# One-hots of the graph matrix for 8 or 10 receiver ranges per VectorE operation

## Chip, cores and metric

The kernel runs on one core of a Trainium2 chip. The metric is the device time of one execution in microseconds; of several runs the median is given.

## What is computed

The reference is a graph network on 12,500 nodes of 64 features and 212,500 edges, sorted by receiver. Cut to what matters:

```python
h = maximum(layernorm(x), 0)
for i in range(3):                         # L0_gnn, relu after the first two
    agg = segment_sum(h[src], dst) / maximum(count(dst), 1)
    h = agg @ Wl[i] + h @ Wr[i] + b[i]
x = x + h
h = maximum(layernorm(x), 0)
e = segment_sum(edge_attr, dst) / maximum(count(dst), 1)
x = x + mlp(concatenate([e, h]))           # three layers, W0, W1, W2
```

The sums over senders are made as matrix products: the graph is written out as a matrix with a small count for each sender and receiver, and all of it is multiplied with the node rows.

## The kernel before

The nodes form 98 blocks of 128 (`NB`), taken as 49 pairs (`HP`). The work has a start and three stages, one for each layer; the edge sums and the last network are woven into the third.

**Start.** The receivers at the heads of the edge tiles are fetched to `heads_row`, copied by VectorE to `heads_f` and spread over the partitions by TensorE (L321) and ScalarE (L324) into `heads`. The node rows come in 14 loads `xb` (L476) through SP's queue; `normed` and `relu_parts` (L201 to L226) apply the layer norm and cut the result into bfloat16 parts. The first matrix is built meanwhile.

**Stage one** does two things at once: it builds the matrix and uses it for the first layer. It runs over 49 passes, `hp` from 0. In pass `hp`, `dense` (L229) makes 98 matmuls at L234 and 98 at L243, whose moving operand is the matrix `m` of this pair of receiver blocks. Between them `woven` (L287) sets "fills" at given shares of the pass: 26 pair steps and a store that make the matrix of pass `hp + 1`, and at shares 0.05 and 0.15 the end of the pass before, `conv`'s `turn` (L260, L264) and `mix` (L269, L273, then L277, L280 on VectorE) followed by `relu_parts`.

**A pair step** (`pair`, L434) treats two receiver ranges. A block has 26 ranges of at most five receivers (`QW`, `WD`), each with up to 128 edges, one edge per partition. For a range, VectorE compares a row of numbers with a number per partition: `c` (L439) has 245 columns and a one where the edge's sender block and receiver fall, `h` (L443) has 128 columns with the sender's place in its block, times a weight of 1 or 256. TensorE multiplies the two (L447), into one half of a PSUM tile `pb` (three of them), and ScalarE casts the pair's result into `m` (L450). `c` and `h` come from the pool `hot` with six buffers each. The numbers `lo`, `weight` and `col` are float32 tiles, one column for each range.

**The index.** `index(j)` (L335) prepares those numbers for four blocks: it scans `heads` (L340, 1664 elements), gathers edges by three indirect DMAs that GpSimd issues (L330), counts on VectorE (L350 to L391), passes five small matmuls (L397) and a transpose (L406) through TensorE, and unpacks the codes (L414 to L426). It is woven in at share 0.6 of each even pass up to 44. Two indices are made in the start.

**Stages two and three** load the stored matrices back (L559) and multiply them with 512 columns at once; they use no one-hots of the edited kind.

**What sets the order.** On TensorE the order is that in which the code issues (`manual_schedule`). On VectorE, ScalarE and the queues the framework's scheduler orders the instructions; each engine then runs its list in order, waiting on semaphores. Tiles come from pools: a tile that takes a buffer waits until its last reader is done, and so does a pool that takes memory of a closed one. Pools `idx`, `hot`, `ln` (for the layer norm), `heads` and `mats` (three matrices `m`) are open through stage one; the pool `row` of the head row is closed early.

Of the kernel before, what the change touches and what calls it, by code (L numbers as in the profile page):

```python
# [9 lines left out]
F32 = mybir.dt.float32  # L10
I32 = mybir.dt.int32
BF16 = mybir.dt.bfloat16
# [3 lines left out]
ALU = mybir.AluOpType  # L16
# [5 lines left out]
P = 128  # L22
D = 64
# [11 lines left out]
QW, Q5 = 26, 24  # L35
WD = 5
# [24 lines left out]
def in_order(  # L61
# [24 lines left out]
    nc = tc.nc  # L86
    NB, T, EP = sz.nb, sz.t, sz.ep
    NL = Wl.shape[0]
    assert NB % 2 == 0
    HP = NB // 2  # L90
    CW = HP * WD
    NG = -(-NB // 4)
    assert EP - sz.e >= EK and CW <= 256

# [33 lines left out]
    with tc.tile_pool(name="setup", bufs=1) as s:  # L128
        ic = iota(s, "ic", CW, 1)
        nc.vector.tensor_copy(iota_c, ic)  # L130
# [4 lines left out]
        q = s.tile([P, 1], F32, name="q")  # L135
# [9 lines left out]
        a = s.tile([P, 1], F32, name="a")  # L145
# [40 lines left out]
    parts = [const.tile([P, NB, 3 * D], BF16, name=f"parts{i}") for i in range(2)]  # L186
# [14 lines left out]
    def normed(pool, xb, n, bufs=None):  # L201

        m = pool.tile([P, n], F32, name="ln_m", bufs=bufs)
        nc.vector.tensor_reduce(m, xb, axis=AX.X, op=ALU.add)
        nc.vector.tensor_scalar(m, m, -1.0 / D, None, op0=ALU.mult)
        c = pool.tile([P, n, D], F32, name="ln_c", bufs=bufs)
        nc.vector.tensor_tensor(c, xb, m[:, :, None].to_broadcast([P, n, D]), op=ALU.add)
        sq = pool.tile([P, n, D], F32, name="ln_sq", bufs=bufs)
        nc.scalar.activation(sq, c, AF.Square)
        v = pool.tile([P, n], F32, name="ln_v", bufs=bufs)  # L210
        nc.vector.tensor_reduce(v, sq, axis=AX.X, op=ALU.add)
        nc.scalar.activation(v, v, AF.Sqrt, bias=eps_t, scale=1.0 / D)
        nc.vector.reciprocal(v, v)
        nc.vector.tensor_tensor(c, c, v[:, :, None].to_broadcast([P, n, D]), op=ALU.mult)
        return c

    def relu_parts(pool, o, to, bufs=None):

        n = o.shape[1]
        nc.scalar.activation(to[:, :, :D], o, AF.Relu)  # L220
        r = pool.tile([P, n, D], F32, name="rest", bufs=bufs)
        nc.vector.scalar_tensor_tensor(
            r, o, 0.0, to[:, :, :D], op0=ALU.max, op1=ALU.subtract
        )
        nc.scalar.copy(to[:, :, D : 2 * D], r)
        nc.vector.tensor_tensor(to[:, :, 2 * D :], r, to[:, :, D : 2 * D], op=ALU.subtract)  # L226
# [76 lines left out]
    with ExitStack() as s:  # L303
        idx = s.enter_context(tc.tile_pool(name="idx", bufs=2))
        ps_b = s.enter_context(tc.tile_pool(name="ps_build", bufs=3, space=PSUM))
        ps_i = s.enter_context(tc.tile_pool(name="ps_idx", bufs=1, space=PSUM))
        hot = s.enter_context(tc.tile_pool(name="hot", bufs=6))
        ln = s.enter_context(tc.tile_pool(name="ln", bufs=1))
        heads = s.enter_context(tc.tile_pool(name="heads", bufs=1)).tile([P, T], F32, name="heads")
        with tc.tile_pool(name="row", bufs=1) as r:  # L310
            heads_row = r.tile([1, T], I32, name="heads_row")
# [6 lines left out]
            for c in range(0, T, 512):  # L318
                n = min(512, T - c)
# [2 lines left out]
                    ph[:, :n], ones[:1, :], heads_f[:, c : c + n], start=True, stop=True  # L322
                )
                nc.scalar.copy(heads[:, c : c + n], ph[:, :n])  # L324
        mats = s.enter_context(tc.tile_pool(name="mats", bufs=3))

        tiles_d = dst.rearrange("(t e) o -> t (e o)", e=P)

# [6 lines left out]
        def index(j):  # L335
# [5 lines left out]
                lower, heads, n0, None, op0=ALU.is_lt, op1=ALU.add, accum_out=tile_of  # L341
# [9 lines left out]
                junk, ends, n0, None, op0=ALU.is_lt, op1=ALU.add, accum_out=in_tile  # L351
# [30 lines left out]
            own = 32 * min(4, NB - 4 * j)  # L382
            for k in range(1, 5):
# [3 lines left out]
                    op1=ALU.is_equal, accum_out=twins[:own, j, k - 1 : k],  # L387
# [8 lines left out]
            for d in range(WD):  # L396
# [11 lines left out]
            nc.vector.tensor_copy(ci, pi[:, 1, :])  # L408
            a = idx.tile([P, P], I32, name="a")
            b = idx.tile([P, P], I32, name="b")  # L410
            lo = idx.tile([P, P], F32, name="lo")
            weight = idx.tile([P, P], F32, name="weight")
            col = idx.tile([P, P], F32, name="col")
            nc.vector.tensor_scalar(a, ci, P - 1, None, op0=ALU.bitwise_and)  # L414
            nc.vector.tensor_copy(lo, a)
            nc.vector.tensor_scalar(
                b, ci, 7, 1, op0=ALU.logical_shift_right, op1=ALU.bitwise_and
            )
            nc.vector.tensor_scalar(weight, b, 255.0, 1.0, op0=ALU.mult, op1=ALU.add)
# [6 lines left out]
            nc.vector.scalar_tensor_tensor(col, a, float(WD), b, op0=ALU.mult, op1=ALU.add)  # L426
            return lo, weight, col

        def build(m, block, codes):

            lo, weight, col = codes
            off = P * (block % 2)

            def pair(q):  # L434
                pb = ps_b.tile([P, 2, 256], F32, name="pb")
                for i in range(2):
                    w = 32 * (block % 4) + q + i
                    c = hot.tile([P, CW], BF16, name="c")
                    nc.vector.tensor_scalar(  # L439
                        c, iota_c, col[:, w : w + 1], None, op0=ALU.is_equal  # L440
                    )
                    h = hot.tile([P, P], BF16, name="h")
                    nc.vector.tensor_scalar(  # L443
                        h, iota_l, lo[:, w : w + 1], weight[:, w : w + 1],
                        op0=ALU.is_equal, op1=ALU.mult,
                    )
                    nc.tensor.matmul(pb[:, i, :CW], h, c, start=True, stop=True)  # L447
                k = WD if q < Q5 else WD - 1
                o = off + WD * q - max(q - Q5, 0)
                nc.scalar.copy(  # L450
                    m[:, :, o : o + 2 * k].rearrange("p h (w d) -> p h w d", d=k),
                    pb[:, :, :CW].rearrange("p w (h d) -> p h w d", d=WD)[:, :, :, :k],
                )

            return [lambda q=q: pair(q) for q in range(0, QW, 2)]
# [26 lines left out]
        with tc.manual_schedule(engines={PE}):  # L482
            codes[1] = index(1)
            m, fills = matrix(0)
            for f in fills:
                f()
            later = []
            for hp in range(HP):
                fills = list(later)
                if hp + 1 < HP:  # L490
                    m_next, more = matrix(hp + 1)
                    fills += [((i + 0.5) / len(more), f) for i, f in enumerate(more)]
                if hp % 2 == 0 and hp // 2 + 2 < NG:
# [12 lines left out]
                if hp + 1 < HP:  # L506
                    m = m_next
            for _, f in later:
                f()


    with ExitStack() as s:
# [4 lines left out]
        n = T // 4  # L517
# [29 lines left out]
    with ExitStack() as s:  # L547
        mats = s.enter_context(tc.tile_pool(name="mats2", bufs=9, reuse_waits="tile"))
# [14 lines left out]
        with tc.manual_schedule(engines={PE}):  # L563
            later = []
            for g in range(NG):
                j0, n = 4 * g, min(4, NB - 4 * g)
# [116 lines left out]
            for g in range(NG):  # L683
                j0, n = 4 * g, min(4, NB - 4 * g)
# [575 lines left out]
```

## Time and profile before

| | |
|---|---|
| median of 3 runs | 3512.63 us (3511.34 to 3512.82) |
| profiled execution | 3514.05 us |
| its span on the core | 3512.3 us, mean granted clock 0.992 |
| TensorE busy | 3350.0 us, 95% of the span |
| VectorE busy | 2111.3 us, 60% |
| ScalarE busy | 1196.0 us, 34% |
| start, to the first L234 | 0 to 104.0 us |
| stage one | 104.0 to 1450.7 us |
| stages two and three | 1450.7 us to the end |

A line of the groups gives source line, engine, operation, output and inputs, shapes and count; then the busy time in all and the mean length of one in ns; then the idle time of the engine just before them and what ended it. A line of the timeline gives the start and the length in us, then the same; a bracket at its end is the engine's wait and what ended it. Busy time is summed without overlap, while lengths of neighbouring operations can overlap, so the distance from start to start tells what one costs its engine.

### The profile page before, as it was taken

The numbers are of one execution on the slowest core, as the hardware profiler recorded it, in microseconds if no ns is written. First come the engines' busy times: TensorE is split into PE (matmuls) and PEld (weight loads), VectorE is DVE, ScalarE is ACT, GpSimd is POOL, SyncE is SP. The second block draws the span as 40 slices with busy tenths as digits, with TensorE's granted clock in tenths as the row PEclk, the third lists the DMA queues.
The fourth block names the chain that finished last, engine by engine and source line by source line (L and its number), as shares of the span: only waits on it lengthen the run. The fifth ranks groups of instructions, "written<-read, shape, count | busy, mean of one in ns | idle before, by whom it ended". The sixth has DMA issues, their size and how long they took to land.

```text
span 3512.3 us, 69396 instructions
## 1 busy us (share of the span) xinstructions
PE 3350.0 (95%) x26430; PEld 2019.0 (57%) x26430; DVE 2111.3 (60%) x9072; ACT 1196.0 (34%) x2101; POOL 750.7 (21%) x482
## 2 busy tenths in 40 slices
PE   1899999999999999999999999979999999999998
PEld 0566777777777777555454545544555555555555
DVE  8999999999999999300000000035556555555554
ACT  4555555555555555100000000022322322322232
POOL 1000000000000000000000000055555565555562
PEclk9999999999999999999999999989999999999999
DMA  2222222332223223645454545455455555555551
GB/s 45 115 116 118 115 116 115 137 129 115 115 120 146 115 111 134 233 155 220 155 212 165 202 176 191 170 218 181 176 182 211 204 206 181 176 183 211 204 193 53
DMA packets 168554, 555.12 MB, mean 158 GB/s; under 512 B 57793, under 2 KB 60386, under 8 KB 161938
## 3 DMA queue, kind: packets, MB, share of 16 engines
q1 hardware_dynamic: 133232, 478.53, 35.7%
q0 software_dynamic: 19648, 66.90, 5.6%
q10 hardware_dynamic: 15330, 5.16, 0.6%
q8 instruction: 208, 3.41, 0.4%
q14 instruction: 136, 1.11, 0.1%
HBM read 389.97 MB, written 160.56 MB: 157 GB/s over the span
## 4 chain that ended last, share of the span: by engine, by line
PE 84%; DVE 10%; issue 4%; DMA 1%; ACT 1%; POOL 0%; ACTq 0%; SPq 0%; DVEq 0%; POOLq 0%
PE p L234 40%; PE p L243 24%; PE pb L447 8%; PE pe L631 5%; DVE h L443 2%; DVE c L439 2%; PE po L273 2%; PE po L269 2%; PE pt L260 2%; DVE own L627 2%; PE ph L666 1%; PE mo L674 1%; DVE lower L340 0%; DVE junk L385 0%; PE mt L659 0%
## 5 line engine op out<-in xcount | busy, mean ns | idle before, releaser
L234 PEld LDWEIGHTS <-parts 128*128 128x128 bf16 x9702 | 937.2, 99 | 584.7 <-issue 46.2
L234 PE MATMUL p<-t,parts 128*128 128x512 fp8e3 (+1 forms) x4900 | 1106.7, 376 | 4.6 <-DMA t<-mat 4.6
L450 ACT CAST m<-pb 128x490 uint16<-128x490 f32 (+1 forms) x1274 | 717.4, 563 | 537.3 <-PE pb L447 534.4
L627 DVE TENSOR_SCALAR own<-iota_l,eplace 128x128 bf16<-128x128 bf16 x1862 | 548.2, 353 | 401.8 <-PE pe L631 401.4
L443 DVE TENSOR_SCALAR h<-iota_l,lo,weight 128x128 bf16<-128x128 bf16 x2548 | 779.8, 306 | 0.0
L439 DVE TENSOR_SCALAR c<-iota_c,col 128x245 bf16<-128x245 bf16 x2548 | 716.5, 281 | 10.9 <-PE pb L447 5.5
L243 PEld LDWEIGHTS <-parts 128*64 128x64 bf16 x9702 | 494.1, 109 | 387.8 <-issue 185.1
L234 PE MATMUL p<-m,parts 128*128 128x256 fp8e3 x4802 | 652.3, 273 | 0.6 <-ACT m L450 0.6
L243 PE MATMUL p<-t,parts 128*64 128x512 fp8e3 (+1 forms) x4900 | 584.4, 378 | 0.0
L447 PE MATMUL pb<-c,h 128*128 128x245 bf16 x2548 | 499.0, 274 | 52.4 <-DVE h L443 35.0
L248 DVE TENSOR_TENSOR agg<-e,p 128x256 f32<-128x256 f32 (+1 forms) x99 | 54.4, 549 | 603.2 <-PE p L243 600.3
L243 PE MATMUL p<-m,parts 128*64 128x256 fp8e3 x4802 | 409.3, 281 | 0.0
L602 POOL DMA_INDIRECT raw<-in_edge_dram,mine x98 | 93.7, 956 | 1124.9 <-DMA t<-mat 1098.6
L447 PEld LDWEIGHTS <-h 128*128 128x128 bf16 x2548 | 205.6, 98 | 204.0 <-DVE h L443 148.9
L613 POOL TENSOR_TENSOR erest<-raw,cut 128x1216 f32<-128x1216 f32 x98 | 244.2, 2492 | 202.2 <-issue 198.1
L631 PE MATMUL pe<-cut,own 128*128 128x192 bf16 x1862 | 227.0, 248 | 34.9 <-DVE own L627 17.5
L631 PEld LDWEIGHTS <-own 128*128 128x128 bf16 x1862 | 151.3, 98 | 166.4 <-issue 58.6
L615 POOL TENSOR_TENSOR cut<-erest,cut 128x1216 bf16<-128x1216 f32 x98 | 244.6, 2496 | 11.2 <-ACT cut L614 2.6
L612 ACT CAST cut<-raw 128x1216 bf16<-128x1216 f32 x98 | 118.1, 1205 | 275.6 <-PE pe L631 266.0
L277 DVE TENSOR_TENSOR o<-po,inv 128x128 f32<-128x128 f32 (+1 forms) x99 | 35.1, 354 | 271.8 <-PE po L273 271.6
L614 ACT CAST cut<-erest 128x1216 bf16<-128x1216 f32 x98 | 118.1, 1205 | 225.6 <-POOL erest L613 225.6
L330 POOL DMA_INDIRECT to<-in_dst_dram,at_i x25 | 23.6, 946 | 709.6 <-DVE at_i L358 595.8
(143 smaller groups left out, 1666.8 us busy)
## 6 DMA issues: line engine op xcount, KB each, us to landing
t<-mat SPq DMA_DIRECT2D x686, 448.0 KB, 6.1
mat<-m SPq DMA_DIRECT2D x49, 3136.0 KB, 10.0
xb<-in_x_dram SPq DMA_DIRECT2D x14, 224.0 KB, 2.7
xr<-in_x_dram ACTq DMA_DIRECT2D x24, 128.0 KB, 2.2
out_dram<-o SPq DMA_DIRECT2D x24, 128.0 KB, 2.0
raw<-in_edge_dram,mine POOLq DMA_INDIRECT x98, 5.4
eto<-in_dst_dram,mine POOLq DMA_INDIRECT x98, 3.7
here<-in_dst_dram ACTq DMA_DIRECT2D x4, 208.0 KB, 5.5
```

The costliest lines, as they stand in the source:

```text
L234: nc.tensor.matmul(p1, rows[:, i, : 2 * D], at(i), start=i == 0, stop=i == NB - 1)
L243: nc.tensor.matmul(p2[half], rows[:, i, 2 * D :], at(i), start=i < 2, stop=i >= NB - 2)
L439: nc.vector.tensor_scalar(c, iota_c, col[:, w : w + 1], None, op0=ALU.is_equal)
L443: nc.vector.tensor_scalar(h, iota_l, lo[:, w : w + 1], weight[:, w : w + 1], op0=ALU.is_equal, op1=ALU.mult,)
L447: nc.tensor.matmul(pb[:, i, :CW], h, c, start=True, stop=True)
L450: nc.scalar.copy(m[:, :, o : o + 2 * k].rearrange("p h (w d) -> p h w d", d=k), pb[:, :, :CW].rearrange("p w (h d) -> p h w d", d=WD)[:, : ...
L612: nc.scalar.copy(cut[:, :, :D], raw)
L613: nc.gpsimd.tensor_tensor(rest, raw, cut[:, :, :D], op=ALU.subtract)
L614: nc.scalar.copy(cut[:, :, D : 2 * D], rest)
L615: nc.gpsimd.tensor_tensor(cut[:, :, 2 * D :], rest, cut[:, :, D : 2 * D], op=ALU.subtract)
L627: nc.vector.tensor_scalar(o, iota_l, place[:, k : k + 1], 1.0 / UNIT, op0=ALU.is_equal, op1=ALU.mult,)
L631: nc.tensor.matmul(state["p"], o, cut[:, k, :], start=k == 0, stop=k == EK - 1)
```

## The change

For each block, VectorE makes the one-hots in three batches of 10, 8 and 8 ranges, each with three operations: one `tensor_tensor` comparison for all `c`, one for all `h`, and one `tensor_tensor` product of `h` with the weights, in place. One operand is the row of numbers, repeated for each range; the other is the code of the range, repeated along the row. Codes now stand twice, in bfloat16, so that they are read as rows of two neighbours; `lo`, `weight` and `col` are twice as long. `CW` becomes 246; the matmul still reads 245 columns. `hot` has two buffers of each kind, each for ten ranges.

Memory is laid out anew: `ln` is now opened after `row` is closed and is closed itself before `mats` is opened, so that `mats` comes to lie where `ln` was, and `ln` where `row` was. The code of the layer norm is moved, not altered.

```diff
-    CW = HP * WD
+    CW = 2 * (-(-HP * WD // 2))
...
-        hot = s.enter_context(tc.tile_pool(name="hot", bufs=6))
-        ln = s.enter_context(tc.tile_pool(name="ln", bufs=1))
+        hot = s.enter_context(tc.tile_pool(name="hot", bufs=2))
...
-        mats = s.enter_context(tc.tile_pool(name="mats", bufs=3))
...
-            lo = idx.tile([P, P], F32, name="lo")
-            weight = idx.tile([P, P], F32, name="weight")
-            col = idx.tile([P, P], F32, name="col")
+            lo = idx.tile([P, P, 2], BF16, name="lo")
+            weight = idx.tile([P, P, 2], BF16, name="weight")
+            col = idx.tile([P, P, 2], BF16, name="col")
+            twice = lambda t: t[:, :, None].to_broadcast([P, P, 2])
...
-            nc.vector.tensor_copy(lo, a)
+            nc.vector.tensor_copy(lo, twice(a))
...
+            cuts = [(0, 10), (10, 18), (18, QW)]
+            ready = {}
+
+            def hots(q0, q1):
+
+                n = q1 - q0
+                w = 32 * (block % 4) + q0
+                pairs = lambda t, k: t.rearrange("p (k t) -> p k t", t=2)[:, None].to_broadcast(
+                    [P, n, k // 2, 2]
+                )
+                own = lambda t, k: t[:, w : w + n, None, :].to_broadcast([P, n, k // 2, 2])
+                split = lambda t: t[:, :n].rearrange("p w (k t) -> p w k t", t=2)
+                c = hot.tile([P, 10, CW], BF16, name="c")
+                nc.vector.tensor_tensor(
+                    split(c), pairs(iota_c, CW), own(col, CW), op=ALU.is_equal
+                )
+                h = hot.tile([P, 10, P], BF16, name="h")
+                nc.vector.tensor_tensor(split(h), pairs(iota_l, P), own(lo, P), op=ALU.is_equal)
+                nc.vector.tensor_tensor(split(h), split(h), own(weight, P), op=ALU.mult)
+                for i in range(n):
+                    ready[q0 + i] = (h[:, i, :], c[:, i, : HP * WD])
 
             def pair(q):
+                for cut in cuts:
+                    if q == cut[0]:
+                        hots(*cut)
                 pb = ps_b.tile([P, 2, 256], F32, name="pb")
                 for i in range(2):
-                    w = 32 * (block % 4) + q + i
-                    c = hot.tile([P, CW], BF16, name="c")
-                    nc.vector.tensor_scalar(
-                        c, iota_c, col[:, w : w + 1], None, op0=ALU.is_equal
-                    )
-                    h = hot.tile([P, P], BF16, name="h")
-                    nc.vector.tensor_scalar(
-                        h, iota_l, lo[:, w : w + 1], weight[:, w : w + 1],
-                        op0=ALU.is_equal, op1=ALU.mult,
-                    )
-                    nc.tensor.matmul(pb[:, i, :CW], h, c, start=True, stop=True)
+                    h, c = ready[q + i]
+                    nc.tensor.matmul(pb[:, i, : HP * WD], h, c, start=True, stop=True)
...
-        def start_rows(a0):
-            n = min(LG, NB - a0)
-            xb = ln.tile([P, n, D], F32, name="xb", bufs=2)
-            nc.sync.dma_start(xb, xv[:, a0 : a0 + n, :])
-            relu_parts(ln, normed(ln, xb, n), parts[0][:, a0 : a0 + n, :])
-
         codes[0] = index(0)
-        for a0 in range(0, NB, LG):
-            start_rows(a0)
+        with tc.tile_pool(name="ln", bufs=1) as ln:
+            for a0 in range(0, NB, LG):
+                n = min(LG, NB - a0)
+                xb = ln.tile([P, n, D], F32, name="xb", bufs=2)
+                nc.sync.dma_start(xb, xv[:, a0 : a0 + n, :])
+                relu_parts(ln, normed(ln, xb, n), parts[0][:, a0 : a0 + n, :])
+        mats = s.enter_context(tc.tile_pool(name="mats", bufs=3))
```

In the changed kernel the comparisons stand at L448 (`c`) and L452 (`h`), the product at L453, the matmul at L464 and the cast at L467; lines below the `hot` pool and above L406 move up by one or two.

More of the change, by code (lines that the diff above doesn't have):

```diff
@@ L418, in index @@
             )
-            nc.vector.tensor_scalar(weight, b, 255.0, 1.0, op0=ALU.mult, op1=ALU.add)
+            nc.vector.tensor_scalar(weight, twice(b), 255.0, 1.0, op0=ALU.mult, op1=ALU.add)
             a = idx.tile([P, P], I32, name="a")
@@ L425, in index @@
             nc.vector.tensor_scalar(b, ci, 14, None, op0=ALU.logical_shift_right)
-            nc.vector.scalar_tensor_tensor(col, a, float(WD), b, op0=ALU.mult, op1=ALU.add)
+            nc.vector.scalar_tensor_tensor(
+                col, twice(a), float(WD), twice(b), op0=ALU.mult, op1=ALU.add
+            )
             return lo, weight, col
@@ L432, in build @@
             off = P * (block % 2)
+            cuts = [(0, 10), (10, 18), (18, QW)]
[11 more added lines that the diff above has]
+                    split(c), pairs(iota_c, CW), own(col, CW), op=ALU.is_equal
+                )
+                h = hot.tile([P, 10, P], BF16, name="h")
[3 more added lines that the diff above has]
+                    ready[q0 + i] = (h[:, i, :], c[:, i, : HP * WD])
             def pair(q):
+                for cut in cuts:
+                    if q == cut[0]:
+                        hots(*cut)
                 pb = ps_b.tile([P, 2, 256], F32, name="pb")
                 for i in range(2):
-                    w = 32 * (block % 4) + q + i
-                    c = hot.tile([P, CW], BF16, name="c")
-                    nc.vector.tensor_scalar(
-                        c, iota_c, col[:, w : w + 1], None, op0=ALU.is_equal
-                    )
-                    h = hot.tile([P, P], BF16, name="h")
-                    nc.vector.tensor_scalar(
-                        h, iota_l, lo[:, w : w + 1], weight[:, w : w + 1],
-                        op0=ALU.is_equal, op1=ALU.mult,
-                    )
-                    nc.tensor.matmul(pb[:, i, :CW], h, c, start=True, stop=True)
+                    h, c = ready[q + i]
+                    nc.tensor.matmul(pb[:, i, : HP * WD], h, c, start=True, stop=True)
                 k = WD if q < Q5 else WD - 1
@@ L451, in pair @@
                     m[:, :, o : o + 2 * k].rearrange("p h (w d) -> p h w d", d=k),
-                    pb[:, :, :CW].rearrange("p w (h d) -> p h w d", d=WD)[:, :, :, :k],
+                    pb[:, :, : HP * WD].rearrange("p w (h d) -> p h w d", d=WD)[:, :, :, :k],
                 )
```

## The prediction, made before the changed kernel was run

> **What bounds the kernel now.** I read the slices of the page first, then the groups, then two windows, then the timeline around one stall. The slices:
>
> ```profile
> PE   1899999999999999999999999979999999999998
> ...
> DVE  8999999999999999300000000035556555555554
> ...
> PEclk9999999999999999999999999989999999999999
> ```
>
> TensorE is at nine tenths all through; VectorE only until about 1400 us, the stage that builds the graph matrix. Only that stage runs the edited code. Its groups:
>
> ```profile
> L443 DVE TENSOR_SCALAR h<-iota_l,lo,weight 128x128 bf16<-128x128 bf16 x2548 | 779.8, 306 | 0.0
> L439 DVE TENSOR_SCALAR c<-iota_c,col 128x245 bf16<-128x245 bf16 x2548 | 716.5, 281 | 10.9 <-PE pb L447 5.5
> ...
> L447 PE MATMUL pb<-c,h 128*128 128x245 bf16 x2548 | 499.0, 274 | 52.4 <-DVE h L443 35.0
> ```
>
> The durations overlap: 281 + 306 = 587 ns per range would be 30.5 us for the 52 ranges of a pass, and a pass takes some 27. The timeline gives the true spacing:
>
> ```profile
> 599.77 0.28 DVE L439 TENSOR_SCALAR c<-iota_c,col 128x245 bf16<-128x245 bf16 x1
> ...
> 599.96 0.30 DVE L443 TENSOR_SCALAR h<-iota_l,lo,weight 128x128 bf16<-128x128 bf16 x1
> ...
> 600.18 0.28 DVE L439 TENSOR_SCALAR c<-iota_c,col 128x245 bf16<-128x245 bf16 x1
> ```
>
> c holds VectorE 0.195 us and h 0.222, so a range costs 0.417. Now two odd passes side by side (columns: window, its length, busy time of PE, PEld, DVE, ACT, POOL):
>
> ```profile
> 697.10:724.50 27.40, 26.48 (x264) 19.61 (x262) 27.15 (x128) 15.68 (x30) 1.89 (x2) 1.00 0.30 123
> ...
> 1240.80:1267.10 26.30, 26.30 (x265) 19.52 (x264) 25.67 (x124) 15.68 (x30) 0.00 (x0) 1.00 0.30 124
> ```
>
> The first loses 0.92 us of PE busy time, the second none: 26.26 us is what TensorE needs when nothing holds it. What held the first:
>
> ```profile
> 711.16 1.94 DVE L340 TENSOR_SCALAR_CACHE_REDUCE lower<-heads,node 128x1664 bf16<-128x1664 f32 x1
> ...
> 713.78 0.56 PE L447 MATMUL pb<-c,h 128*128 128x245 bf16 x2 [0.92 <-DVE c L439]
> ```
>
> The 1.94 us count of the next index stands between one-hots, and the pair's matmul waits. So TensorE bounds this stage, and VectorE, nearly full, adds short stalls.
>
> **What the Trainium skill says.** "VectorE: DVE Perf Modes", The perf-mode tier table, gives tensor_tensor on bf16 in SBUF two results a cycle at best. The trace has no such operation: every tensor_tensor in it has a float32 side. "Vector Engine (DVE) Microarchitecture Reference", 5.1 Performance modes, asks for 2-byte types, innermost step 1 and over one element, and says that rows of two elements and a row read again do run at two. The built operands are of that kind: iota in runs of 246 or 128 repeated per range, each code as a row of two repeated. 5.2 of that page, Measured stream behaviour, charges a source that hops every 4-byte word up to 1.73 ns a column; whether re-reading one word counts so no run shows, though L207, which re-reads one float32 per group, took 417 ns beside 418 to 458 for same-size operations without that.
>
> **The change, part by part.** Rate: L226 takes 282 ns for 128 elements and 618 for 448, so 1.05 ns an element at one a cycle; its spacing of 0.20 us for 128 leaves 67 ns fixed. c at 245 elements fits two a cycle: 245 x 0.525 + 67 = 195.
>
> 1. Removed: 26 c and 26 h per block, 26 x 0.417 = 10.84 us.
> 2. Added, at 0.525 ns: c for 10, 8, 8 ranges, 1.36 + 1.10 + 1.10; h compare and h multiply 0.74 + 0.61 + 0.61 each; the multiply waits for the compare's end, about 0.09 (306 - 222) three times. Sum 7.7 us. Bounds: 14.3 + 0.3 at one element a cycle; below, 7.4 without the waits. I take 7.7. A pass of two blocks sheds 6.2 us of VectorE.
> 3. lo, weight and col twice as long: +0.3 to +0.5 us per index, 25 of them, under TensorE's work. Without that cover, 13 us in all.
> 4. TensorE's order and matmuls, and ACT's casts, are unchanged. So a pass can only come down to its floor. By the starts of L234 in the trace, passes 0 to 47 take 1322.5 us. Floors: 26.26 without an index, 27.18 with one (its five small matmuls, the transpose and a 0.25 us wait), 25 x 26.26 + 23 x 27.18 = 1281.6. **At most 40.9 us** to win: some 26 in passes 0 to 9, 15 in the odd passes 11 to 35 at 1.16 each.
> 5. New wait: with two buffers a batch's c waits until TensorE has read the batch before the last. Behind it on VectorE are agg (L248), L277, L280 and the index chain. In a floor pass the batches are first read at 0.45, 6.83, 10.83, 14.84, 19.18 and 23.54 us. By hand on the built order, with an index: agg at 0.2 to 0.6, batch two ready 2, counts and the 1.94 us scan to 5.5, L277 from 5.6, a wait for the gather (issued about 3.7, 2.5 to land) to 6.3, batch three ready 9.6 (read 10.8), batch four 14.2 (14.8), batch five 16.7 (19.2), batch six 22.7 (24.4, the index moves it), next batch one 26.2 (27.6). All are in time, the tightest by 0.6 us. I keep 3 us for stalls: bounds 0 and, if 0.7 us were lost in each of 23 passes, 16. Loop: -38.
> 6. Start. Before, VectorE ends the layer norm at 97.3, and the first dense matmul comes 6.7 later:
>
> ```profile
> 97.63 5.81 PE L447 MATMUL pb<-c,h 128*128 128x245 bf16 x14 [0.57 <-DVE h L443]
> 104.01 1.01 PE L234 MATMUL p<-m,parts 128*128 128x256 fp8e3 x4 [0.57 <-ACT m L450]
> ```
>
> Three things move. (a) The ln tiles now lie where the head row lay, so SP's x loads wait for the head matmuls (last ends 16.4 us, before L204 started at 10.4), and VectorE, out of setup work by 14, idles until the heads are copied: about +2. (b) The built order puts seven head scans before the norm's end, not three, and 3 more chains at least partly: 4 x 1.94 + about 9 = 16.7 us; against that two batches (5) replace 39 ranges (39 x 0.417 = 16.3): +5. (c) mats overlies ln, so all 26 casts of matrix 0 come after the norm, not 7. ACT spaces them 0.465 (95.65 to 96.12 below), 12.1 us, and twice a multiply is queued behind the next c, which waits for a buffer, 1.3 to 2 us: 15.7 in place of 6.7, and some 0.5 to the first cast and matmul: about +10.
>
> ```profile
> 95.65 0.57 ACT L450 CAST m<-pb 128x490 uint16<-128x490 f32 x1 [0.33 <-PE pb L447]
> 96.12 0.56 ACT L225 CAST parts<-rest 128x448 bf16<-128x448 f32 x1
> ```
>
> Sum +17; bounds +10 (a hidden, no queue) and +24. Index work done early wins nothing later, since TensorE bounds the passes.
> 7. After 1450 us no line changes; SP's t loads wait on other addresses, and I cost that at nothing: behind it lie nine buffers, and the existing first wait there is 4.6 us. If that grew, it would double at worst.
>
> Sum: -38 + 17 = **-21 us**. The profiled execution took 3514.05 (span 3512.3), 1.4 over the median 3512.63. 3512.6 - 21 = 3492 us.
>
> **Rivals.** *Start hidden* (A): the batches make the start's VectorE work shorter than I count, start about +2, loop -39: 3476. For it: VectorE is the engine of the first 100 us. Against: the casts cannot start earlier. *Edges stall* (B): 0.7 to 1 us at one late batch in each pass, loop about -15: 3512 to 3516. For it: a margin of 0.6 us in step 5. Against: VectorE's slack of 5 us a pass recovers. *Slow reads* (C), the one that ends slower: the repeated two-element rows run at one a cycle. Then a pass costs VectorE 2 x 14.6 + 5.3 (other work: 27.4 less 52 x 0.417, less half a microsecond idle) = 34.5 against 27.2 now, 48 x 7.3 = 350, plus the start: about 3880. It decides from 10.7 us a block (26.7 - 5.3 over two); the 1.73 ns price, two elements to a column, would give about 12.2 and so 3650. For it: no such operation in the trace. Against: the page's measured rows. That the change does not do what it says is excluded by the built program: 3 c, 3 h and 3 multiplies a block.
>
> **Numbers.** Forecast (start +10 to +24, loop -25 to -41) 0.62; A 0.10; B 0.14; C 0.14. Measurements of this kernel tell about 0.2% (7 us) from no change. Faster: forecast, A and 0.04 of B, 0.76; same 0.10 from B; slower C. Own range of the forecast 3481 to 3512; with A and most of B 3475 to 3514, which leaves out C and a rest.
>
> **What would show it.** c of 2460 elements near 1.4 us apart from the next, not 2.65; odd passes at 26.26 from the first on; the first L234 at about 121 us; L467's casts all after the last L225. Wrong: passes over 27.5, waits of L464 for the multiply in every pass, or a first L234 near 105.

## The result, and the profile after

| | before | after |
|---|---|---|
| median | 3512.73 us (4 runs, 3511.34 to 3516.27) | 3566.57 us (4 runs, 3564.33 to 3567.49) |
| ratio, 95% interval | | 1.0151, 1.0133 to 1.0168 |
| span of the profiled execution | 3512.3 us | 3562.5 us |
| VectorE busy | 2111.3 us | 1831.2 us |
| first L234 | 104.0 us | 124.7 us |
| passes 0 to 47 | 1322.5 us | 1352.8 us |
| pass 48 | 24.2 us | 23.8 us |
| from there to the end | 2061.7 us | 2061.2 us |

The kernel became slower by 1.5%, where 0.6% faster was forecast. The spans differ by 50.2 us: 20.7 in the start, 30.3 in passes 0 to 47, -0.3 in pass 48 and -0.5 behind it. A pass is counted from its first L234 to that of the next. The slices of the changed kernel:

```profile
PE   0699999999999999999999999989999999999998
...
DVE  8777777777677676400000000026555565555554
```

VectorE got its room: 7 tenths where it had 9. TensorE has next to no work in the first slice and needs longer to the end of the stage. The groups of stage one, by shape, show that the batches cost what was forecast:

```profile
L448 DVE TENSOR_TENSOR c<-iota_c,col 128x1968 bf16<-128x1968 bf16 x195 | 230.5, 1182 | 108.8 <-PE pb L464 108.7
...
L448 DVE TENSOR_TENSOR c<-iota_c,col 128x2460 bf16<-128x2460 bf16 x97 | 139.7, 1440 | 61.9 <-PE pb L464 61.8
...
L453 DVE TENSOR_TENSOR h<-h,weight 128x1280 bf16<-128x1280 bf16 x97 | 79.9, 824 | 2.6
...
L363 DVE TENSOR_SCALAR place<-to,node 128x128 f32<-128x128 int32 x20 | 5.7, 286 | 85.6 <-DMA to<-in_dst_dram,at_i 85.6
```

From 1968 to 2460 elements the time grows by 258 ns, 0.524 ns an element, half of the 1.05 ns that the prediction took from L226. What is new is the idle time of the last line: `place` works for 5.7 us in all, and VectorE waits 85.6 us before it for the gathered receivers `to`. In the kernel before, VectorE never waited before the same operation:

```profile
L365 DVE TENSOR_SCALAR place<-to,node 128x128 f32<-128x128 int32 x25 | 7.0, 278 | 0.0
```

Pass by pass (windows of three passes; length, then busy time of PE, PEld, DVE, ACT, POOL; clock, DMA share, GB/s):

```profile
691.40:718.70 27.30, 27.05 (x271) 19.82 (x270) 19.88 (x42) 15.69 (x30) 0.00 (x0) 1.00 0.28 119
718.70:747.80 29.10, 26.77 (x264) 19.27 (x262) 21.36 (x48) 15.56 (x30) 2.83 (x3) 1.00 0.30 119
...
1291.40:1317.70 26.30, 26.30 (x264) 19.44 (x263) 17.36 (x28) 15.68 (x30) 0.00 (x0) 1.00 0.30 124
```

The even pass stands at its floor of 27.24 us. The odd pass with the three gathers (POOL x3) takes 29.1, and the odd pass without them 26.3. Over passes 0 to 47 the floors (26.33 without an index, 27.24 with one) sum to 1284.8 us; 68.0 us are stalls, 67 of them in the 20 odd passes 1 to 39. The timeline of the odd pass from 718.70:

```profile
718.62 0.32 SPq L483 DMA_DIRECT2D mat<-m  x1
...
721.74 0.15 DVE L356 TENSOR_SCALAR at_i<-begins 128x1 int32<-128x1 f32 x1
...
722.17 0.94 POOL L328 DMA_INDIRECT to<-in_dst_dram,at_i  x1 [52.27 <-DVE at_i L356]
...
724.40 0.29 DVE L277 TENSOR_TENSOR o<-po,inv 128x128 f32<-128x128 f32 x1 [0.27 <-PE po L273]
...
728.89 0.29 DVE L363 TENSOR_SCALAR place<-to,node 128x128 f32<-128x128 int32 x1 [4.19 <-DMA to<-in_dst_dram,at_i]
729.09 0.28 DVE L280 TENSOR_TENSOR o<-o,po 128x128 f32<-128x128 f32 x1
...
729.40 0.31 ACT L220 ACTIVATE parts<-o 128x128 bf16<-128x128 f32 x1 [3.89 <-DVE o L280]
729.62 0.55 ACT L467 CAST m<-pb 128x490 uint16<-128x490 f32 x1
730.22 0.37 PE L464 MATMUL pb<-c,h 128*128 128x245 bf16 x2 [1.51 <-ACT m L467]
...
732.13 0.39 PE L464 MATMUL pb<-c,h 128*128 128x245 bf16 x2 [0.77 <-DVE h L453]
```

Read it as a chain. The 3.1 MB store of the finished matrix is issued at the pass's start. VectorE, ahead of its old place, reaches `at_i` 3 us later, so the gather is issued while the store runs. `place` is a few operations further in VectorE's order, after the 1.94 us scan and directly behind L277; VectorE stands 4.19 us before it, waiting for the gather. Behind it stand L280 and the next batch of `c`. ScalarE's L220 waits for L280, and the casts that free `pb` stand behind L220. TensorE then loses 1.51 us to a late cast and 0.77 to a late product. Over passes 0 to 47 these two waits of TensorE make 46 of the 67 us (us, times, longest):

```profile
PE pb L464 <- ACT m L467: 31.9, 20, 2.9
PE pb L464 <- DVE h L453: 13.9, 18, 0.8
```

In the kernel before, in the odd pass from 697.1, `at_i` came 14 us into the pass, when the store had ended, and `place` 16.7 us behind it:

```profile
711.10 0.15 DVE L358 TENSOR_SCALAR at_i<-begins 128x1 int32<-128x1 f32 x1
...
727.76 0.28 DVE L365 TENSOR_SCALAR place<-to,node 128x128 f32<-128x128 int32 x1
```

Why the gather is late is in the DMA view, cut at 727.3 us (queue: packets, MB, share of 16 engines). From 719.4 to 727.3:

```profile
q1 hardware_dynamic: 128, 3.21, 100.8%
...
to<-in_dst_dram,at_i POOLq DMA_INDIRECT x1, 6.7
```

From 727.3 to 729.7:

```profile
q0 software_dynamic: 96, 0.20, 23.5%
```

The store's packets fill all 16 engines up to 727.3, and of the gathers' queue q0 not one packet moves until then, 5 us after the issue. The gather lands after 6.7 us; in the pass of the kernel before it was 2.6. It is the same in each odd pass from 3 to 39: the trace's first packet of q0 comes 5.1 to 5.2 us after the issue.

The start is the other part. The layer norm's last product, the first cast into `m` and the matmul behind it:

```profile
107.75 0.63 DVE L226 TENSOR_TENSOR parts<-rest,parts 128x448 bf16<-128x448 f32 x1 [0.63 <-ACT parts L225]
108.46 1.98 ACT L467 CAST m<-pb 128x490 uint16<-128x490 f32 x4 [0.74 <-DVE parts L226]
109.08 1.04 PE L464 MATMUL pb<-c,h 128*128 128x245 bf16 x4 [53.29 <-ACT m L467]
```

TensorE had its first `pb` tiles full for 53 us. No cast could run, because `m` lies where the layer norm's tiles were; all 26 casts then run between 108.5 and 124.6.

### The profile page after: what moved, and what is told of

Its sections match the earlier page's. It is cut to its first block, busy times and chain, and to the rows that moved or that the text cites. A ratio compares the mean times of both kernels' runs of the same rounds, so it can differ in the third digit from the quotient of the medians.

```text
span 3562.5 us, 63699 instructions
## 1 busy us (share of the span) xinstructions
PE 3352.2 (94%) x26430; PEld 2017.5 (57%) x26430; DVE 1831.2 (51%) x4858; ACT 1191.5 (33%) x2101; POOL 750.2 (21%) x482
## 4 chain that ended last, share of the span: by engine, by line
PE 63%; issue 30%; DVE 4%; POOL 2%; DMA 1%; ACT 0%; SPq 0%; POOLq 0%; DVEq 0%; ACTq 0%
PE p L234 32%; PE p L243 17%; PE pe L647 5%; PE pb L464 2%; DVE own L643 2%; PE ph L682 1%; PE po L273 1%; PE po L269 1%; PE pt L260 1%; PE mo L690 1%; POOL ends L328 1%; POOL to L328 1%; DMA to<-in_dst_dram,at_i 0%; POOL of L328 0%; PE mt L675 0%
## 5 line engine op out<-in xcount | busy, mean ns | idle before, releaser
L234 PEld LDWEIGHTS <-parts 128*128 128x128 bf16 x9702 | 940.6, 99 | 592.3 <-issue 46.9
L234 PE MATMUL p<-t,parts 128*128 128x512 fp8e3 (+1 forms) x4900 | 1106.0, 376 | 4.3 <-DMA t<-mat 4.3
L467 ACT CAST m<-pb 128x490 uint16<-128x490 f32 (+1 forms) x1274 | 710.6, 564 | 476.9 <-PE pb L464 471.2
L643 DVE TENSOR_SCALAR own<-iota_l,eplace 128x128 bf16<-128x128 bf16 x1862 | 567.2, 364 | 383.6 <-PE pe L647 383.2
L234 PE MATMUL p<-m,parts 128*128 128x256 fp8e3 x4802 | 661.8, 276 | 0.8 <-ACT m L467 0.8
L464 PE MATMUL pb<-c,h 128*128 128x245 bf16 x2548 | 489.8, 275 | 104.5 <-ACT m L467 85.6
L448 DVE TENSOR_TENSOR c<-iota_c,col 128x1968 bf16<-128x1968 bf16 (+1 forms) x294 | 372.8, 1268 | 170.7 <-PE pb L464 170.5
L464 PEld LDWEIGHTS <-h 128*128 128x128 bf16 x2548 | 201.9, 99 | 249.6 <-issue 200.3
L277 DVE TENSOR_TENSOR o<-po,inv 128x128 f32<-128x128 f32 (+1 forms) x99 | 35.3, 356 | 372.3 <-PE po L273 372.3
L453 DVE TENSOR_TENSOR h<-h,weight 128x1024 bf16<-128x1024 bf16 (+1 forms) x294 | 215.6, 733 | 6.1
L452 DVE TENSOR_TENSOR h<-iota_l,lo 128x1024 bf16<-128x1024 bf16 (+1 forms) x294 | 214.3, 729 | 0.0
```

The source lines that it names most:

```text
L234: nc.tensor.matmul(p1, rows[:, i, : 2 * D], at(i), start=i == 0, stop=i == NB - 1)
L448: nc.vector.tensor_tensor(split(c), pairs(iota_c, CW), own(col, CW), op=ALU.is_equal)
L452: nc.vector.tensor_tensor(split(h), pairs(iota_l, P), own(lo, P), op=ALU.is_equal)
L453: nc.vector.tensor_tensor(split(h), split(h), own(weight, P), op=ALU.mult)
L464: nc.tensor.matmul(pb[:, i, : HP * WD], h, c, start=True, stop=True)
L467: nc.scalar.copy(m[:, :, o : o + 2 * k].rearrange("p h (w d) -> p h w d", d=k), pb[:, :, : HP * WD].rearrange("p w (h d) -> p h w d", d=WD ...
```

## The experiments

My theory: the loop loses about 67 us because the gather falls into the store and VectorE's list waits at `place`; the start loses about 20 through the memory layout. The rivals: two buffers of one-hots are too few, or the batches stall TensorE by themselves. Line numbers of variants differ by up to two from the changed kernel's. Each was timed beside the kernel before, whose median was then 3513.2 to 3513.8 us; ratios are to it.

### The store later in the pass

```diff
-            return m, fills + [store]
+            return m, fills, store
...
-                fills = list(later)
+                fills = list(later) + [(0.45, store)]
```

> The changed kernel with one edit: the store of a finished matrix is issued at share 0.45 of the pass that uses it, not at the end of the pass before. VectorE's order stays the same. Theory (the gather for the index is slowed from 2.5 us to 6 and more by the 3.1 MB store that starts 3.5 us before it, and VectorE, ScalarE and TensorE queue behind the wait for it): to<-in_dst_dram lands in 2.5 us again, the 86 us of waiting at L363 shrink to under 10, odd passes fall from 28.4 to 33.2 us to about 26.3, and the kernel gains 60 to 71 us: about 3500. Rival (two buffers of one-hots are too few, and the batches wait for each other): nothing changes, 3567.

Measured: 3581.82 us, ratio 1.019 (1.0173 to 1.0207). This experiment missed. The store is still issued as soon as the last cast is done, 0.02 to 0.03 us ahead of the pass (0.05 in the changed kernel), although the code names it later. So the collision stayed (L363 waits 87.0 us). The 26 fills that are left also move to other shares, and all passes became 0.4 to 0.5 us longer, perhaps by that; it was not tried apart. The run tells nothing of the theory, except that the store is not moved by naming it later while the scheduler orders SP's queue.

### `place` on GpSimd

```diff
-            nc.vector.tensor_scalar(place, to, n0, 7.0, op0=ALU.subtract, op1=ALU.min)
+            nc.gpsimd.tensor_scalar(place, to, n0, 7.0, op0=ALU.subtract, op1=ALU.min)
```

> The changed kernel with one edit: place (L363) is computed on GpSimd, so that GpSimd and not VectorE waits for the gathered receivers. The store stays where it was. Theory: the gather still takes 6 us and more, but L277 and L280 stand next to each other on VectorE, ScalarE's casts are not held, and odd passes come to 26.3 to 27.0 us: about 3500 to 3510. If the slow gather hurt by another way than VectorE's queue, nothing changes. Rival of too few buffers: 3567.

Measured: 3519.16 us (3517.27 to 3522.26), 47 us less than the changed kernel, ratio to before 1.0017 (1.0010 to 1.0024), and 9 above the range. The waits in stage one (engine, line, waited for: us, times, longest):

```profile
POOL place L363 <- DMA to<-in_dst_dram,at_i: 47.3, 20, 5.0
DVE behind L369 <- POOL place L363: 42.5, 20, 3.2
```

The gather is still late, but now GpSimd waits, and VectorE only at L369, which stands later in its list. The odd passes 1 to 47 fall from a mean of 29.1 to 27.0 us. So VectorE's wait in order is the main way by which the late gather reaches TensorE. In passes 0 to 47 no wait for a late cast of `m` is left at L464, since L280 no longer stands behind `place`; 12.6 us for late products are, as VectorE still waits at L369. The start is 5.8 us longer (first L234 at 130.5), which was not followed up.

### Three buffers of one-hots

```diff
-        hot = s.enter_context(tc.tile_pool(name="hot", bufs=2))
+        hot = s.enter_context(tc.tile_pool(name="hot", bufs=3))
...
-        mats = s.enter_context(tc.tile_pool(name="mats", bufs=3))
+        mats = s.enter_context(tc.tile_pool(name="mats", bufs=2))
```

The third buffer takes the room of the third matrix.

> The changed kernel with three buffers of each kind in the pool of one-hots, and two matrices in mats instead of three, which makes the room. The place of L363 between L277 and L280 and the store stay. Theory of the gather: VectorE is still held for 3.5 to 5.5 us with L280 behind it, ScalarE's relu and the casts still queue; a batch more in stock helps only where the multiply was late as well, so at most a third of the 65 us of stalls goes: 3545 to 3567. Rival of too few buffers: the stalls go, 3500.

Measured: 3553.32 us (3552.45 to 3554.13), ratio 1.0115. L363 waits as long as in the changed kernel (86.7 us), and odd passes have a mean of 28.7. In passes 0 to 47 L464 no longer waits for a late product, but 39.9 us for late casts (31.9 in the changed kernel). So a third buffer covers the late batch and not the casts behind L220. It brings 13 us, 2.4 of them in the start, and the rival of too few buffers falls as the main cause.

### The layer norm's tiles back in their place

```diff
+        ln = s.enter_context(tc.tile_pool(name="ln", bufs=1))
...
+        mats = s.enter_context(tc.tile_pool(name="mats", bufs=2))
...
-        with tc.tile_pool(name="ln", bufs=1) as ln:
+        if True:
...
-        mats = s.enter_context(tc.tile_pool(name="mats", bufs=3))
```

Three matrices do not fit beside open layer norm tiles and the batches, so this takes two.

> The changed kernel with the memory of the start as before: ln is opened ahead of the head row and mats ahead of the first index; mats has two matrices instead of three, since three do not fit beside the larger one-hots. Theory of the start (20 us are lost there because the x loads wait for the head row's memory and all casts for the norm's): the first L234 comes at 100 to 106 us in place of 124.7, the passes stay as in the changed kernel, about 3547. Rival (the start is late because of the index work and the batches, not of the memory): first L234 at 118 or later, 3560 or more.

Measured: 3543.81 us (3541.73 to 3546.55), ratio 1.0085: 23 us less than the changed kernel. The first L234 is at 85.5 us, earlier than the 100 to 106 expected. Pass 0 then takes 47.4, waiting for the norm's last rows, and pass 1 starts at 132.8, in place of 152.9 (before: 137.1). L365 (`place` here) still waits 86.3 us. With batches, the start's loss is the layout's, apart from the loop's. The number of matrices is not the reason: a run below has the old layout with three of them, and pass 1 starts at 132.4.

### The layout alone, with the old one-hots

Against the kernel before:

```diff
-        ln = s.enter_context(tc.tile_pool(name="ln", bufs=1))
...
-        mats = s.enter_context(tc.tile_pool(name="mats", bufs=3))
...
+        with tc.tile_pool(name="ln", bufs=1) as ln:
...
+        mats = s.enter_context(tc.tile_pool(name="mats", bufs=3))
```

> The one-hots of the kernel before (one operation each, six buffers), with only the changed memory layout: the layer norm's tiles over the head row, the matrices over the layer norm's. If the layout alone costs the start: casts of the first matrix all after the norm's last tile, first L234 at 115 to 125 us in place of 104, passes as before (1322 us for 0 to 47), time 3525 to 3535. If the start's loss comes from the batches: first L234 at 104 to 108 and 3513 to 3517.

Measured: 3515.15 us (3514.22 to 3516.68), ratio 1.0004 (0.9995 to 1.0013). The start is as expected; its end on the timeline:

```profile
105.14 0.63 DVE L226 TENSOR_TENSOR parts<-rest,parts 128x448 bf16<-128x448 f32 x1 [0.63 <-ACT parts L225]
105.84 3.87 ACT L448 CAST m<-pb 128x490 uint16<-128x490 f32 x8 [0.74 <-DVE parts L226]
...
124.64 1.01 PE L234 MATMUL p<-m,parts 128*128 128x256 fp8e3 x4 [0.57 <-ACT m L448]
```

The time is not. I had expected 3525 to 3535. Passes 0 to 9 took 273.7 us in place of 292.9: what the start loses with the old one-hots, the first passes give back. That fits the index work, of which seven head scans lie before the first L234 here and three in the kernel before. With batches less comes back: in the two batch kernels below with the index at share 0.35, the changed layout has its first L234 39.0 us later than the old one and is still 15.1 us behind at the start of pass 3; from there on both layouts stand at the floor.

### Stores in pairs

```diff
+            held[hp] = m
+
             def store():
-                nc.sync.dma_start(mat[hp], m)
+                if hp % 2 == 0:
+                    for k in (hp, hp - 1)[: 1 + (hp > 0)]:
+                        nc.sync.dma_start(mat[k], held[k])
...
-        with tc.manual_schedule(engines={PE}):
+        with tc.manual_schedule(engines={PE, mybir.EngineType.SP}):
```

Two stores run in each even pass and none in an odd one. The second edit makes SP's queue follow the code's order, so that the stores stay where the code has them; it was not run alone. VectorE's order is the changed kernel's, with `place` between L277 and L280.

> The changed kernel, with the store of every odd matrix held back until the next, even one is built: both are then issued together at the end of odd passes, so that no store runs while the index's gather is under way early in an odd pass. VectorE's order is that of the changed kernel. Collision (the gather waits for the 3.1 MB store, and VectorE's queue behind L363 with it): the gather lands in 2.5 to 3.5 us as in the kernel before, waits of L363 for it fall from 86 us to under 10, odd passes from a mean of 29.2 us to 26.3 to 27, the time to 3500 to 3512. Rival (the batches themselves, or VectorE's order, hold the odd passes, and the gather's wait only covers it): odd passes stay near 29 and the time near 3567. Between them, if the two stores in a row disturb the even passes: even passes over 27.24, time 3515 to 3540.

Measured: 3502.66 us (3501.45 to 3503.43), ratio 0.9969 (0.9957 to 0.9982). An even and an odd pass, in the windows:

```profile
660.30:687.60 27.30, 27.05 (x273) 19.79 (x270) 19.89 (x42) 15.69 (x30) 0.00 (x0) 1.00 0.56 236
687.60:713.90 26.30, 26.30 (x264) 19.44 (x262) 21.53 (x48) 15.59 (x30) 2.83 (x3) 1.00 0.03 9
```

The DMA share is 0.56 in the even pass and 0.03 in the odd, and the odd pass with its three gathers stands at 26.3 us. Its timeline:

```profile
690.65 0.15 DVE L356 TENSOR_SCALAR at_i<-begins 128x1 int32<-128x1 f32 x1
...
691.08 0.94 POOL L328 DMA_INDIRECT to<-in_dst_dram,at_i  x1 [50.12 <-DVE at_i L356]
...
693.32 0.29 DVE L277 TENSOR_TENSOR o<-po,inv 128x128 f32<-128x128 f32 x1 [0.27 <-issue]
...
693.52 0.30 DVE L363 TENSOR_SCALAR place<-to,node 128x128 f32<-128x128 int32 x1
...
693.75 0.28 DVE L280 TENSOR_TENSOR o<-o,po 128x128 f32<-128x128 f32 x1
```

The gather is issued at the same point of the pass, 3.5 us in, and `place` has its data 2.4 us later; the first packet of q0 comes 1.6 us after the issue, in place of 5.2. In stage one its waits are

```profile
DVE place L363 <- DMA to<-in_dst_dram,at_i: 3.3, 3, 1.5
```

in place of 85.6. Passes 0 to 47 take 1284.8 us, the sum of the floors; the first L234 is at 124.7 as in the changed kernel. The one cost is at the end: pass 48, with two stores beside it, takes 28.8 us in place of 23.8. This decides for the collision. The batches, and VectorE's order without a store beside the gather, do not hold the passes.

### The index at another share of the pass

```diff
-                    fills.append((0.6, lambda j=j: codes.__setitem__(j, index(j))))
+                    fills.append((0.35, lambda j=j: codes.__setitem__(j, index(j))))
```

> The changed kernel with one number changed: the index is woven in at share 0.35 of the even pass, not 0.6, so that VectorE's order has at_i about the middle of the even pass, after the pass's store has ended, and place two batches after at_i, not between L277 and L280. Stores are where they were. Collision theory: gathers land in 2.5 to 3.5 us, no wait of L363 over 1 us, odd passes 26.3, even 27.2, first L234 124.7, pass 48 23.8 as in the changed kernel: 3567 less the 67 us of the odd passes = 3496 to 3503. Rival (it was the pairing of the stores that helped in another way, such as bandwidth for SP in the odd passes): odd passes stay over 28, time over 3540.

Measured: 3503.13 us (3501.71 to 3504.15), ratio 0.9972 (0.9960 to 0.9983). Here it is the gather that moves, to 18.7 us into an even pass (that from 609.8 below), and `place` stands 5.1 us behind `at_i`:

```profile
628.21 0.15 DVE L356 TENSOR_SCALAR at_i<-begins 128x1 int32<-128x1 f32 x1
...
633.34 0.28 DVE L363 TENSOR_SCALAR place<-to,node 128x128 f32<-128x128 int32 x1
```

No wait for a gather is left in stage one; odd passes take 26.33 us, even 27.49. Even passes take 0.25 more than with paired stores, and L404 in them waits 0.73 us for the count (16.9 us in 23 times, in place of 5.9); whether that is all of it was not tried. Two edits, of the store and of the gather, remove the same 67 us from the odd passes.

### Both parts mended: two tries and a better one

> Two partial undoings together: the layer norm's memory laid out as before the change (with two matrix buffers, as it else doesn't fit) and place on GpSimd in place of VectorE. Alone they gave -23 and -47 us against the changed kernel. If start and loop are separate parts of the loss, they add: 3567 - 23 - 47 = 3497, with the span of 3490 to 3503, first L234 near 85, odd passes near 27. If they share a cause (early index work moved from the start to the loop), less: 3510 to 3519.

```diff
+        ln = s.enter_context(tc.tile_pool(name="ln", bufs=1))
...
-            nc.vector.tensor_scalar(place, to, n0, 7.0, op0=ALU.subtract, op1=ALU.min)
+            nc.gpsimd.tensor_scalar(place, to, n0, 7.0, op0=ALU.subtract, op1=ALU.min)
```

`place` on GpSimd with the layer norm's tiles back and two matrices, as in the two diffs above: 3506.00 us (3501.35 to 3508.86), ratio 0.9977. Odd passes take 27.1, as expected; but pass 0 took 55.9 us, 8.5 more than with the tiles back alone, and that is about the 9 us missing to 3497. Why it did was not followed up.

> The memory laid out as in the kernel before, three matrix buffers, stores in pairs as in the other run, and batches of 4 ranges so that all fits. Fixed costs rise: 7 batches of three operations a block, about 21 x 0.067 us and seven multiplies that wait, in place of 9 x 0.067 and three, so about 1.2 us more of VectorE a block than the batches of 10, 8 and 8. If layout and gather make the loss: first L234 at 95 to 105 us, odd passes 26.3 to 27, even 27.2, time 3480 to 3500. If the batch form itself stalls TensorE: odd passes 28 and more, time over 3515.

```diff
-            cuts = [(0, 10), (10, 18), (18, QW)]
+            cuts = [(q, min(q + 4, QW)) for q in range(0, QW, 4)]
```

With tiles of four ranges, paired stores, the old layout and three matrices: 3503.92 us (3500.59 to 3506.40), ratio 0.9972. The first L234 is at 98.5, odd passes take 26.9, even 27.3; passes 0 and 1 take 33.9 and 33.0. Against the 26.33 of the paired stores, the smaller batches lose TensorE about half a microsecond in an odd pass, no more. The run missed its range by 4 us.

> The same share of 0.35, and the memory laid out as in the kernel before, with two matrix buffers. If the loss has just these two parts, start and collision, first L234 is near 86, pass 1 starts near 133 (152 in the changed kernel), and all passes from 1 stand at 26.3 and 27.2: 3500 less 19 = 3478 to 3488. If the start's index work only moves into the first passes: 3490 to 3502.

```diff
+        ln = s.enter_context(tc.tile_pool(name="ln", bufs=1))
...
-                    fills.append((0.6, lambda j=j: codes.__setitem__(j, index(j))))
+                    fills.append((0.35, lambda j=j: codes.__setitem__(j, index(j))))
```

The index at share 0.35 and the layer norm's tiles back, with two matrices: **3485.76 us (3484.25 to 3487.24), ratio 0.9922 (0.9908 to 0.9935)**, the best of all, 81 us below the changed kernel and 27 below the one before. Its passes 0 and 1 and two later ones:

```profile
85.50:129.40 43.90, 29.95 (x255) 20.69 (x255) 40.77 (x102) 23.24 (x45) 4.03 (x4) 0.84 0.26 91
129.40:163.50 34.10, 29.08 (x265) 20.45 (x264) 27.49 (x87) 15.56 (x30) 7.71 (x8) 0.90 0.29 109
...
648.50:676.00 27.50, 26.77 (x271) 19.78 (x269) 22.65 (x56) 15.67 (x30) 3.26 (x3) 1.00 0.31 125
676.00:702.30 26.30, 26.30 (x264) 19.44 (x262) 17.97 (x34) 15.67 (x30) 0.00 (x0) 1.00 0.29 124
```

The time is in its range, but by a somewhat different way. Pass 1 starts at 129.4, but it takes 34.1 us, where I had expected 26.3: VectorE is busy for 27.5 of it, and GpSimd runs 8 operations there, where an ordinary pass with an index has 3. This is index work that the other layout does before the first pass (three head scans lie before the first L234 here, seven there). One gather of it falls into pass 1's store: it lands after 8.0 us, L365 waits 5.6 us for it, and TensorE loses 4.0 us to the late cast behind, so the collision itself comes back once. From the start of pass 3 on, at 191.7 us, every pass is at 26.3 or 27.5; with the index at the same share and the changed layout pass 3 starts at 206.8.

### Control: the kernel before with the index at that share

> Control: the kernel before with the index at share 0.35 instead of 0.6. There VectorE is full, so a shift of the index's place should not remove its work from between the one-hots: 3508 to 3518, odd passes near 27.4 and even passes 27.2. If the shift is worth something without the batches as well, the time falls below 3505, and that part of the gain of the shifted batch kernels isn't the batches'.

Measured: 3502.03 us (3501.20 to 3502.52), ratio 0.9969 (0.9956 to 0.9981). I had expected no change. From pass 10 to 35 a pair of passes takes 54.07 us in place of 54.60, which makes 7 of the 11 us: odd passes 27.12 in place of 27.42, even ones 26.95 in place of 27.18. So part of the gain of the shifted batch kernels is the shift's own. What the batches add beside it in the old layout, with two matrices in place of three, is 3502.0 - 3485.8 = 16 us.

## Why the prediction was wrong

**Steps 1 and 2 held.** A batch of ten ranges of `c` was costed at 1.36 us; in the timeline of the start, `c` at 120.22 is followed by the next operation at 121.58. The price of two a cycle, which I took from the Trainium skill, "Vector Engine (DVE) Microarchitecture Reference", 5.1 Performance modes, and "VectorE: DVE Perf Modes", The perf-mode tier table, is what this trace shows. The first page states it for two elements per partition and for a row read again; that a row of two elements read again counts as well was my reading, and the 0.524 ns an element bears it out. VectorE's busy time fell by 280 us, where 6.2 in each of 49 passes would make 304. The rival of slow reads (3880) is out.

**Steps 3 and 4 held.** By their durations, the three longer code tiles take 0.28 us more per index, just below the 0.3 to 0.5. Floors were forecast at 26.26 and 27.18 us, 1281.6 in all; with paired stores the passes run at 26.33 and 27.24, 1284.8. So the loop's gain of 38 us exists, and that kernel shows it: 1322.5 - 1284.8 = 37.7.

**Step 5 failed**, at the words "a wait for the gather (issued about 3.7, 2.5 to land) to 6.3". The issue was right (3.5 us into the pass). The landing was taken from the kernel before, where the gather ran 14 us into the pass, after the store. At 3.5 us the store is under way, and the gather needed 6.7, so that `place` ran at 10.2 and not at 6.3. Batch three, costed ready at 9.6 against a need at 10.8, was ready at 13.4. I had given these waits 3 us, with 16 as their bound; they took 67. The number was in the profile. The store is issued at the pass's start and takes 10.0 us, and the view of L330 in the kernel before ends with

```profile
DMA to landing us min/median/max: 2.4/2.5/6.3
```

The 6.3 is the gather `to` of passes 4 and 8. There it was issued 3.75 us into the pass, under the store, close to the 3.5 us of the changed kernel's odd passes. VectorE did not wait for it, as `place` came 6.5 us after the issue in its list, with L277 and L280 ahead of it. I took the median, moved an instruction to another time, and kept a duration that had been measured at the old time. I also followed only the batch as a victim: L280 is queued behind `place` too, and through it L220 and the casts on ScalarE, which cost TensorE the larger of the two waits, 31.9 us against 13.9.

**Step 6 held in kind**, +20.7 in place of +17, within its bounds of +10 and +24. First L234 124.7 against 121, all casts after the last L225, as said. The norm ends at 108.4 in place of 97.3, 11 us later where (a) and (b) made 7, and the dense matmul comes 16.3 behind it in place of 6.7, the 10 us of (c). The layout alone gives 124.6. "Index work done early wins nothing later" did not hold: the layout that has more of it in the start gains back 24 of its 39 us over passes 0 to 2 (82.3 us, against 106.1 with the old layout, both with the index at 0.35). How much of that is index work and how much the norm, which in the old layout ends only in pass 0, was not separated.

**Step 7 held**: 2061.2 us against 2061.7.

The sum without the failed term is what the kernel with paired stores shows: -37.7 + 20.7 = -17, and with the 4.6 us that pass 48 grows, -12; measured spans 3500.0 against 3512.3. The rival of stalled edges had the right kind of place, one late batch in a pass with an index, but 0.7 to 1 us for it, where 3.4 were lost on the mean. The case in which the gather meets the store was among none of my rivals, and the one that ended slower was on another mechanism.

What stays open is why q0's packets follow those of the store. The runs show the order, and the paired run, with VectorE's list unchanged, that VectorE's work is not what delays them. Where the order is made no run here shows. Nor was it tried why the shift alone helps the kernel before.

## What to carry to other kernels

When an engine becomes faster, its list moves against everything that keeps its time: look up what each transfer it triggers will then run beside, and price the transfer there, not where it ran before. If the profile has a longest landing far above the median, find out what ran beside it. A wait that is harmless with 16 us between issue and use decides the pass when the scheduler closes that gap, and the victims are all that stand behind it in order, on its engine and on those that wait for them. A gain that was forecast and is missing may still be there: edits of the index's share and of the layout turned 54 us lost into 27 us won, of which the share alone wins 11 without the batches.

## What had not been expected of the hardware

- An indirect gather of 128 x 128 words moved no packet for 5 us while a 3.1 MB store was running on another queue, and landed after 6.7 us, not 2.6. Between 200 and 1300 us of the execution the median was 6.5, against 2.5 in the kernel before.
- The clock granted to TensorE was below 1 in pass 0: 0.72 with 35.2 us of work in 55.8 (`place` on GpSimd, tiles back), 0.84 with 30.0 in 43.9 (the best kernel), 0.95 with 29.5 in 33.1 (the kernel before). Much waiting does not explain all of it, as the changed kernel's pass 0 has 0.91 with 27.9 in 28.2. What sets it was not tried.
